# Folding the second entry's w2 on VectorE with operands in PSUM, in a conditioned transformer block on one Trainium2 core

## The chip, the core and the metric

The kernel runs on one core of a Trainium2 chip. The core has TensorE (matrix products into PSUM), VectorE (element-wise steps and the reads that add a product to its destination), ScalarE, called ACT in the profile (activations and copies), GpSimd, called POOL (element-wise sums in SBUF), and SyncE, called SP, which issues transfers. The metric is the device time of one execution in microseconds.

## The reference

For two batch entries of 2048 rows with 512 features, everything in f32:

```
emb = silu(t) @ ada_w + ada_b                 # six rows of 512 for each batch entry
shift_msa, scale_msa, gate_msa, shift_mlp, scale_mlp, gate_mlp = split(emb, 6)
norm = ln(x) * (1 + scale_msa) + shift_msa
h    = gelu(norm @ ssm_w1 + ssm_b1)           # 512 x 512, the error-function gelu
x    = x + gate_msa * (h @ ssm_w2 + ssm_b2)   # 512 x 512
n2   = ln(x) * (1 + scale_mlp) + shift_mlp
hf   = gelu(n2 @ ff_w1 + ff_b1)               # 512 x 1024, the tanh gelu
x    = x + gate_mlp * (hf @ ff_w2 + ff_b2)    # 1024 x 512
```

## The kernel before, in words

The 4096 rows are cut into eight blocks of 512 rows, numbered 0 to 7; blocks 0 to 3 belong to the first batch entry, 4 to 7 to the second. Each block passes four products, named in the tiles: hA (norm by w1, then gelu), oA (by w2, added to x), hC (n2 by fw1, then gelu) and oC (by fw2, added to x). The order of the work on each engine is the order in which the Python code issues it. Around block i the stages come as hC_i ("products"), oA_{i+1}, oC_i, hA_{i+2}, and then hC_{i+1}.

Every product is computed with fewer multiplications at the price of sums: a matrix is cut into quarters 11, 12, 21, 22, seven products P1 to P7 of quarters or sums of quarters are formed, and their results are added into the quarters of the output. `sums_of_second` (lines 397 to 404) forms four such sums for a right-hand weight: s0 = 12 - 11, s1 = 22 - s0, 12 = 22 - 12 and s2 = 21 - s1. For the hC products of later blocks a longer program is used: `HK_B` lists twenty sums of the sixteen input registers of n2 ("forms"), `HK_P` the 26 products in their order, each with the PSUM bank that it uses and the outputs that read it. In `HK_B` GpSimd forms most sums (L1184); those named in `beside` are formed by VectorE (L1180), one operand of each having been copied to PSUM by ACT (L773, `copied_registers`, one tile for register pair 3 and, if register 17 is among them, one for pair 1).

Work that isn't a matrix product is hung into the product stages by `hook(hooks, places, ops)`: after the product at a place has been issued and its result's read has been issued, the steps hooked there are issued. In `group` the places are named "P1", "P2", "P6", "P5", "P7", "P3", "P4" and count the seven positions in that order. The hA groups of blocks 3 and later, which are called with the order `CARRIED`, compute P1, P5, P6, P2, P7, P3, P4 in these positions, so steps hooked at "P5" follow the product P2. hA_0 uses the order `FIRST` and its places carry the products' own names: P1, P2, P5, P6, P7, P3, P4. In the 26 products of hC the places are the numbers of the products; in `residual_in_all_leaves` (oC of blocks 2, 3 and 5) they are "0a", "0b" to "6a", "6b", the two halves of seven rounds.

In a CARRIED hA group P1 goes to a PSUM bank "y", which ACT copies to a bank "x" (L564); P5 and P6 are read by ACT (L814), P2 by ACT with gelu (L824), P7 by VectorE into its destination (L833) and then ACT with gelu (L834), P3 by VectorE (L836) and ACT (L837), and P4 by ACT (L840). P1, P6, P7 and P4 accumulate in the same bank "y", so each of them has to wait for the read of the one before.

The gate of each batch entry is multiplied into the weight instead of the output. For w2 and the second entry this happens around block 2 (`refold2`; i = 2, which is also one of the blocks in `SEVEN`): w2 is loaded anew at "0a" of oC_2 (`load_w`), the gate row (`gsb_2_1`, loaded during oA_3) is copied into a PSUM tile by ACT (`take_gate`, L374) at "P5" of hA_4, and four folds (L434, VectorE, one 128x512 slice of w2 each, the other operand the gate in PSUM) are hooked at "P5", "P7", "P3" and "P4"; `sums_of_second` follows on GpSimd at "P4" (L386). At "P5" the row of b2 is loaded into the buffer that the gate row had (`gate_bias`), and during hC_3, at products 5, 8 and 12, three VectorE steps multiply it by the gate (L1158, L1159, L1160). w2's new operands are first read in oA_4.

Two LayerNorm steps of later blocks are touched too. `sums_on_act` gives the row sums of block i+3 as four ACT activations with an accumulator (L604), each followed by a short accumulator read; `squares_on_act` (L616) gives the squares during the next block's hC products; `root` forms `ve` on VectorE (L640) and then r = ve to the power of -1/2 on GpSimd (L641); `steps` refines r on VectorE (L681 to L689). In hA_0 the batch statistics of one quarter of block 1 are taken on VectorE (`mixed_stats`, L587 and L588), the rest on ACT.

The PSUM pool `ps_t` has two buffers; the register copies, the gate and the small tile of `steps` come from it.

Of the kernel before, what the change touches and what calls it, by code (L numbers as in the profile page):

```python
# [36 lines left out]
F32 = mybir.dt.float32  # L37
AF = mybir.ActivationFunctionType
ALU = mybir.AluOpType
# [101 lines left out]
def kernel(  # L141
# [196 lines left out]
    def gate_rows_of(g):  # L338
        pa = rows_of(g)
        r = w2_t[:, 2 * P : 3 * P] if g == 2 else w2_t[:, 3 * P : 4 * P]  # L340
        nc.vector.tensor_tensor(r, pa[:, :P], gate_b[g], ALU.add)
        gate_rows[g] = r
# [28 lines left out]
    def take_gate(g, b):  # L371

        pg = ps_t.tile([P, D], F32, tag="t", name=f"pgate_{g}_{b}")
        nc.scalar.copy(pg, gate_rows[g, b])  # L374
        gate[g, b] = pg
# [53 lines left out]
    def weight_of_second(w_sb, s, gt, engs, cut=1, sum_eng=nc.gpsimd):  # L429

        K = w_sb.shape[1]

        def fold(k):
            engs[k % len(engs)].tensor_tensor(w_sb[:, k, :], w_sb[:, k, :], gt() if callable(gt) else gt, ALU.mult)  # L434

        ops = [lambda k=k: fold(k) for k in range(K)]
        lo, hi = w_sb[:, : K // 2, :], w_sb[:, K // 2 :, :]
        q = {
            "11": lo[:, :, : D // 2],
            "12": lo[:, :, D // 2 :],  # L440
            "21": hi[:, :, : D // 2],
            "22": hi[:, :, D // 2 :],
        }
        s = thirds(s)
        return second_operands(q, s), ops + sums_of_second(q, s, sum_eng, cut)

    pair_t = fw2_t[:, :2].rearrange("p a s k d -> p (a s k d)").rearrange(
        "p (s k q d) -> p s k q d", s=3, k=KD // 2, q=2
    )
# [118 lines left out]
    def hook(hooks, places, ops):  # L568

        for n, op in enumerate(ops):  # L570
            hooks.setdefault(places[min(n, len(places) - 1)], []).append(op)


    class Norm:
# [192 lines left out]
        def copied_registers(self, ks):  # L767


            copied = {}  # L770
            for k in ks:
                t = ps_t.tile([P, C, 2, HT // C], F32, tag="t", name=f"copy{self.name}_{k}")
                nc.scalar.copy(t, self.nT[:, :, k * P : (k + 1) * P].rearrange("p a (h r) -> p a h r", h=2))  # L773
                copied |= {2 * k + col: t[:, :, col] for col in range(2)}
            return copied
# [569 lines left out]
    def run(ops):  # L1345
        for op in ops:
            op()
# [89 lines left out]
    hook(hooks, ("P1",), n1_sums[2:3])  # L1437
    on_act, on_dve = n1[1].mixed_stats()
    hook(hooks, ("P1",), on_act)
    hook(hooks, ("P2",), on_dve)  # L1440
    hook(hooks, ("P6",), [n1[1].root, lambda: gate_rows_of(2)] + n1_sums[3:])
    hook(hooks, ("P6",), [n1[1].rest] + [lambda c=c: n1[1].normal(c) for c in range(2)])
    hook(hooks, ("P7",), [ssm_gate, gb2_0, lambda: seed("oA_0", b2_bc, 0), lambda: apart_row(b2_bc, nc.gpsimd)] + fold2(0, 1))
    hook(hooks, ("P3",), fold2(1, 2) + [lambda: n1[1].turn(0)] + fold2(2, 4))
# [151 lines left out]
    for i in range(1, NBLK):  # L1596
# [36 lines left out]
            hook(hooks, (17, 19, 21, 23), [lambda c=c: n2[i + 1].turn(c) for c in range(C)])  # L1633
            hook(hooks, (23,), [n2[i + 1].move])
        if nx2 and i > 1:
            hook(hooks, (0,) if ahead else (7,) if unread_stats else (2,), [n1[i + 2].root])
            at = (3, 3, 4, 4, 5, 6) if ahead else (11, 12, 12, 13, 13, 14) if unread_stats else (8, 9, 10, 11, 12, 13)
            hook(hooks, at, n1[i + 2].steps())
        if i == 2:
# [121 lines left out]
        if refold2:  # L1761
            b = (i + 2) // PER_B
            hook(hooks, ("0a",) if seven else ("P1",), [lambda: load_w("w2", w2, w2_sb)])
            w2_ops, w2_fold = weight_of_second(w2_sb, w2_s, (lambda: gate[2, b]) if seven else gate_rows[2, b], (nc.vector,))
            if not seven:
                hook(hooks, ("R2", "R4", "R4", "P3"), w2_fold[:KD])
        if ahead:
            hook(hooks, ("0a",) if seven else ("P1",), [lambda: load_x(i + 2)])
# [16 lines left out]
        if nxt:  # L1785
            def form(engs, beside=()):

                fb[i + 1] = n2[i + 1].registers()
                copied = n2[i + 1].copied_registers((3, 1) if 17 in beside else (3,)) if beside else None
                return sums_of_registers(HK_B, fb[i + 1], engs, copied, beside)  # L1790
# [14 lines left out]
        if not last:  # L1805
            store(i, 1)
        if nx2:
            begin = lambda: run(form((nc.gpsimd,), (19, 12, 7) if refold5 else (19, 17, 12, 11, 2, 7)))
        else:
            begin = lambda: None  # L1810

# [15 lines left out]
            hook(hooks, ("P5",) * 6 + ("P7", "P7", "P3"), folds)  # L1827
        if refold2:
            def bias_2():
                take_gate(2, b)  # L1830
                gb[2], multiply_2 = gate_bias(2, b, b2, f"gb2_{b}")
                return multiply_2()

            found["gb2"] = None
            hook(hooks, ("P5",), [lambda: found.update(gb2=bias_2())])
            if seven:
                hook(hooks, ("P5", "P7", "P3", "P4"), w2_fold[:KD])
            hook(hooks, ("P4",), w2_fold[KD:])
            late_bias = [lambda n=n: found["gb2"][n]() for n in range(3)]
            w2_leaf, late_sums = leaves_of_w2(w2_sb, w2_s, (nc.gpsimd, nc.gpsimd))  # L1840
        unread_stats = []
        if i + 3 < NBLK:
            on_act = i + 4 < NBLK
            st = n1[i + 3].sums_on_act() if on_act else n1[i + 3].stats()
            unread_stats = n1[i + 3].squares_on_act() if on_act else []
            hook(hooks, ("P7", "P7", "P4") if refold5 else ("P5", "P7", "P3", "P4"), st)
        if ahead:
            n2[i + 2] = Norm(i + 2, 2)
            last_stats = n2[i + 2].stats()
# [50 lines left out]
```

## Time and profile before

| | |
|---|---|
| median of 3 runs | 582.67 us (582.5 to 582.76) |
| profiled execution | 582.45 us, its span 580.7 us |
| TensorE busy | 572.8 us (99%) |
| VectorE busy | 450.8 us (78%) |
| GpSimd busy | 435.9 us (75%) |
| ACT busy | 292.5 us (50%) |
| mean granted TensorE clock | 0.998 of full speed |

The span is the time from the first to the last instruction; the rest of the execution's time lies around it. Times in rows of the profile count from the span's start, in microseconds unless marked ns. In a row of a timeline the first number is the start, the second how long the merged instructions lasted, then come engine, line of the kernel, operation, output and inputs, and in brackets the idle time of the engine before it with what ended it. In a row of the chain of waits stand start, length, engine, output and line; DVEq, ACTq and SPq are the instruction queues of VectorE, ACT and SyncE. In a row of groups stand the busy time and the mean ns of one, then the idle time before them. A matrix product x8 is one of the seven products of a group: eight matmuls of 128x256.

### The profile page before, as it was taken

The numbers are of one execution on the slowest core, as the hardware profiler recorded it, in microseconds if no ns is written. First come the engines' busy times: TensorE is split into PE (matmuls) and PEld (weight loads), VectorE is DVE, ScalarE is ACT, GpSimd is POOL, SyncE is SP. The second block draws the span as 40 slices with busy tenths as digits, with TensorE's granted clock in tenths as the row PEclk, the third lists the DMA queues.
The fourth block names the chain that finished last, engine by engine and source line by source line (L and its number), as shares of the span: only waits on it lengthen the run. The fifth ranks groups of instructions, "written<-read, shape, count | busy, mean of one in ns | idle before, by whom it ended". The sixth has DMA issues, their size and how long they took to land.

```text
span 580.7 us, 10061 instructions
## 1 busy us (share of the span) xinstructions
PE 572.8 (99%) x3425; PEld 514.1 (89%) x3425; DVE 450.8 (78%) x954; ACT 292.5 (50%) x573; POOL 435.9 (75%) x453
## 2 busy tenths in 40 slices
PE   8999999999999999999999999999999999999997
PEld 4888888888899889998899988998889998899896
DVE  4968898986878586975869877986757597887677
ACT  3727457705652875448734588335655332741520
POOL 1665449999949879789998989998993955369351
PEclk9999999999999999999999999999999999999999
DMA  8977333204205403373032921243230250031002
GB/s 332 388 220 251 99 74 90 92 37 145 61 14 156 169 40 74 104 241 128 1 91 54 338 98 24 51 122 125 82 108 2 109 145 2 1 74 72 1 2 72
DMA packets 26831, 62.30 MB, mean 107 GB/s; under 512 B 5104, under 2 KB 6172, under 8 KB 25116
## 3 DMA queue, kind: packets, MB, share of 16 engines
q1 hardware_dynamic: 22768, 55.87, 29.7%
q10 hardware_dynamic: 4012, 5.79, 3.9%
q8 instruction: 27, 0.44, 0.3%
q14 instruction: 24, 0.20, 0.1%
HBM read 35.94 MB, written 9.97 MB: 79 GB/s over the span
## 4 chain that ended last, share of the span: by engine, by line
PE 92%; DVE 4%; DMA 2%; issue 1%; ACT 0%; SPq 0%; DVEq 0%; ACTq 0%
PE px_hC L1260 10%; PE py_hA L550 9%; PE pv_hC L1260 8%; PE py_hC L1260 8%; PE py_oA L550 5%; PE py_oC L973 5%; PE pv_hA L550 4%; PE pl_oC_P_y L1021 4%; PE pl_oC_A_y L1111 4%; PE py_oA L908 4%; PE pl_oC_B_y L1111 3%; PE py_hC L550 2%; PE pv_oA L550 2%; PE py_oC L550 2%; PE pl_oC_P_v L1021 2%; PE px_hA L550 2%
## 5 line engine op out<-in xcount | busy, mean ns | idle before, releaser
L641 POOL TENSOR_TENSOR r<-ve,minus_half 128x4 f32<-128x4 f32 x16 | 17.2, 1074 | 53.6 <-DVE ve L640 46.6
L752 ACT ACTIVATE nT<-nT,mod,mod 128x512 f32<-128x512 f32 x32 | 23.4, 803 | 46.1 <-DMA nT<-blocks 32.0
L1184 POOL TENSOR_TENSOR forms<-forms 128x256 f32<-128x256 f32 x56 | 42.1, 751 | 4.2 <-DVE forms L1180 0.7
L1260 PE MATMUL py_hC<-forms,fw 128*128 128x256 f32 x168 | 41.2, 380 | 0.5 <-DVE hClo L1277 0.5
L1277 DVE TENSOR_TENSOR hClo<-hClo,py_hC 128x512 f32<-128x512 f32 x42 | 28.5, 684 | 10.5 <-ACT hClo L1274 8.2
L704 ACT ACTIVATE nT<-x,nmr,rstd 128x512 f32<-128x512 f32 x36 | 26.8, 804 | 19.5 <-DVE nmr L689 16.9
L1260 PEld LDWEIGHTS py_hC<-forms,fw 128*128 128x128 f32 x168 | 31.6, 190 | 5.5 <-DVE hClo L1277 1.2
L386 POOL TENSOR_TENSOR hSC<-hClo,hChi 128x512 f32<-128x512 f32 (+1 forms) x16 | 19.2, 1206 | 20.7 <-ACT hChi L1255 19.1
L587 DVE BATCH_NORM_STATS2 st<-x 128x6 f32<-128x512 f32 x42 | 28.4, 675 | 4.9 <-DMA x<-in_x_dram 4.8
L1277 DVE TENSOR_TENSOR hChi<-hChi,pv_hC 128x512 f32<-128x512 f32 x35 | 23.2, 679 | 10.8 <-ACT hChi L1274 5.1
L1255 ACT ACTIVATE hClo<-hClo,colsT 128x256 f32<-128x256 f32 x56 | 25.3, 498 | 5.3 <-DVE hClo L1277 5.1
L1260 PE MATMUL px_hC<-forms,fw 128*128 128x256 f32 x112 | 27.6, 379 | 0.0
L752 ACT ACTIVATE x<-x,mod 128x512 f32<-128x512 f32 x24 | 17.6, 802 | 19.1 <-DMA x<-blocks 19.1
L715 DVE STREAM_TRANSPOSE blocks<-nT 128x512 f32<-128x512 f32 x36 | 24.2, 694 | 2.8 <-ACT nT L704 2.8
L386 POOL TENSOR_TENSOR hClo<-hClo 128x512 f32<-128x512 f32 (+1 forms) x23 | 26.1, 1137 | 0.0
L1255 ACT ACTIVATE hChi<-hChi,colsT 128x256 f32<-128x256 f32 x56 | 25.1, 495 | 1.9 <-DVE hChi L1277 1.9
L1274 ACT ACTIVATE hChi<-py_hC 128x512 f32<-128x512 f32 x14 | 7.6, 595 | 34.3 <-PE py_hC L1260 34.2
L1260 PEld LDWEIGHTS px_hC<-forms,fw 128*128 128x128 f32 x112 | 21.3, 190 | 2.9
L1274 ACT ACTIVATE hClo<-px_hC 128x512 f32<-128x512 f32 x21 | 12.5, 596 | 22.2 <-PE px_hC L1260 18.6
L550 PE MATMUL py_hA<-x,w 128*128 128x256 f32 x96 | 22.7, 379 | 0.0
L1277 DVE TENSOR_TENSOR hChi<-hChi,px_hC 128x512 f32<-128x512 f32 x28 | 19.0, 680 | 4.5 <-ACT hClo L1274 2.1
L1260 PE MATMUL px_hC<-forms,fw_s 128*128 128x256 f32 x84 | 20.7, 381 | 0.0
(513 smaller groups left out, 1913.2 us busy)
## 6 DMA issues: line engine op xcount, KB each, us to landing
x<-in_x_dram SPq DMA_DIRECT2D x13, 1024.0 KB
out_dram<-x SPq DMA_DIRECT2D x14, 512.0 KB
x<-blocks SPq DMA_DIRECT2D x96, 64.0 KB
nT<-blocks SPq DMA_DIRECT2D x88, 64.0 KB
ada<-in_L_cond_ada_w_dram SPq DMA_DIRECT2D x5, 1024.0 KB
fw<-in_L_cond_ff_w_dram SPq DMA_DIRECT2D x2, 2048.0 KB
nT<-blocks ACTq DMA_DIRECT2D x56, 64.0 KB
w<-in_L_cond_ssm_w_dram SPq DMA_DIRECT2D x2, 1024.0 KB
```

Of the source, the lines that this page charges most:

```text
L386: eng.tensor_tensor(out[:, r], a[:, r], b[:, r], f)
L550: nc.tensor.matmul(ps[b][j * apart][:, j, :], lhs(p, j, k), rhs(p, j, k), start=(fresh and j * (not apart) == 0 and k == 0), stop=(p in (" ...
L587: nc.vector.bn_stats(st, xs[self.i][:, c, :])
L704: nc.scalar.activation(t, x_c, AF.Identity, bias=self.nmr[:, c : c + 1], scale=self.rstd[:, c : c + 1])
L752: nc.scalar.activation(dst, src, AF.Identity, bias=shift, scale=scale)
L973: yield lambda j=j, k=k: nc.tensor.matmul(ps[BANK[p]][:, j, :], hops(p, j, k), wops[p][:, k, :], start=False, stop=(k == kdim - 1), skip_g ...
L1021: nc.tensor.matmul(t[:, n, :], hops.leaves[p][f][:, k, :], leaf_wops[p][f][:, k, :], start=room not in started, stop=(f in ("P2", "P3", "P ...
L1111: nc.tensor.matmul(rooms[g, b][:, at[p], :], hops.leaves[p][f][:, k, :], leaf_wops[p][f][:, k, :], start=(g, b) not in started, stop=(f in ...
L1184: eng.tensor_tensor(reg[d], reg[a], reg[b], ALU.add if f == "+" else ALU.subtract)
L1255: nc.scalar.activation(h, h, AF.Gelu_apprx_tanh, bias=fb1T[:, m : m + 1])
L1260: nc.tensor.matmul(ps[b][:, j, :], fa[ra][:, j * P : (j + 1) * P], fb[rb].rearrange("p a (c q) -> p c a q", q=Q), start=(fresh and j == 0) ...
L1277: nc.vector.tensor_tensor(dest(d), dest(d), ps[b], op)
```

## The change

All of it concerns the refold of w2 for the second entry, and two LayerNorm steps.

- `take_gate` for this refold is hooked at "5b" of oC_2, one stage earlier than "P5" of hA_4.
- The folds go by quarters of w2 in the order 12, 11, 22, 21, all four hooked at "P1" of hA_4. The fold of 12 writes its result into the PSUM tile that held the register copies (`room`); the others write in place.
- The four sums move from GpSimd to VectorE, each with one operand in `room`: s0 = room - 11 and 12 = 22 - room at "P5"; ACT then copies 22 into `room` at "P7", s1 = room - s0 follows at "P3"; ACT copies 21 into `room` at "P3", and s2 = room - s1 follows at "P4".
- Of the sums in `HK_B` for block 3, registers 19, 12 and 7 stay on VectorE; 17, 11 and 2 go to GpSimd, and only one register copy is made.
- ACT's four row sums for block 5 are hooked at "P2", "P6", "P5", "P7" of hA_4 in place of "P5", "P7", "P3", "P4".
- `root` of blocks 4 and 5, in the hC products of blocks 2 and 3, moves from product 7 to product 9, behind the reads of products 8 and 9.
- In hA_0 the VectorE batch statistics of block 1 move from "P2" to the head of "P6", behind the reads of P5 and P6.

```diff
+    def weight_beside(w_sb, s, gt, room):
+
+        K, F, s = w_sb.shape[1] // 2, D // 2, thirds(s)
+        h = w_sb.rearrange("p (h k) (q f) -> p h q k f", h=2, q=2)
+        q = {f"{j + 1}{n + 1}": h[:, j, n] for j in range(2) for n in range(2)}
+
+        def fold(n):
+            out = room() if n == "12" else q[n]
+            c = slice(0, F) if n[1] == "1" else slice(F, D)
+            nc.vector.tensor_tensor(out, q[n], gt()[:, c].unsqueeze(1).to_broadcast([P, K, F]), ALU.mult)
+
+        def beside(out, a, b):
+            return lambda: nc.vector.tensor_tensor(out, a or room(), b or room(), ALU.subtract)
+
+        def copied(n):
+            return lambda: nc.scalar.copy(room(), q[n])
+
+        sums = [beside(s[0], None, q["11"]), beside(q["12"], q["22"], None), copied("22"), beside(s[1], None, s[0])]
+        sums += [copied("21"), beside(s[2], None, s[1])]
+        return second_operands(q, s), [lambda n=n: fold(n) for n in ("12", "11", "22", "21")], sums
...
-                t = ps_t.tile([P, C, 2, HT // C], F32, tag="t", name=f"copy{self.name}_{k}")
+                t = found["copies"] = ps_t.tile([P, C, 2, HT // C], F32, tag="t", name=f"copy{self.name}_{k}")
...
-    hook(hooks, ("P2",), on_dve)
-    hook(hooks, ("P6",), [n1[1].root, lambda: gate_rows_of(2)] + n1_sums[3:])
+    hook(hooks, ("P6",), on_dve + [n1[1].root, lambda: gate_rows_of(2)] + n1_sums[3:])
...
-            hook(hooks, (0,) if ahead else (7,) if unread_stats else (2,), [n1[i + 2].root])
+            hook(hooks, (0,) if ahead else (9,) if unread_stats and not fold else (7,) if unread_stats else (2,), [n1[i + 2].root])
...
-            w2_ops, w2_fold = weight_of_second(w2_sb, w2_s, (lambda: gate[2, b]) if seven else gate_rows[2, b], (nc.vector,))
-            if not seven:
+            if seven:
+                hook(hooks, ("5b",), [lambda: take_gate(2, b)])
+            if seven:
+                room = lambda: found["copies"].rearrange("p a h r -> p (a h r)").rearrange("p (k f) -> p k f", k=KD // 2)
+                w2_ops, w2_fold, w2_sums = weight_beside(w2_sb, w2_s, lambda: gate[2, b], room)
+            else:
+                w2_ops, w2_fold = weight_of_second(w2_sb, w2_s, gate_rows[2, b], (nc.vector,))
...
-            begin = lambda: run(form((nc.gpsimd,), (19, 12, 7) if refold5 else (19, 17, 12, 11, 2, 7)))
+            begin = lambda: run(form((nc.gpsimd,), (19, 12, 7) if refold5 or refold2 else (19, 17, 12, 11, 2, 7)))
...
             def bias_2():
-                take_gate(2, b)
+                if not seven:
+                    take_gate(2, b)
...
             if seven:
-                hook(hooks, ("P5", "P7", "P3", "P4"), w2_fold[:KD])
-            hook(hooks, ("P4",), w2_fold[KD:])
+                hook(hooks, ("P1",), w2_fold)
+                hook(hooks, ("P5", "P5", "P7", "P3", "P3", "P4"), w2_sums)
+            else:
+                hook(hooks, ("P4",), w2_fold[KD:])
...
-            hook(hooks, ("P7", "P7", "P4") if refold5 else ("P5", "P7", "P3", "P4"), st)
+            hook(hooks, ("P7", "P7", "P4") if refold5 else ("P2", "P6", "P5", "P7") if refold2 else ("P5", "P7", "P3", "P4"), st)
```

## Prediction, made before the changed kernel ran

> **What bounds the kernel now.** I read the page first, then TensorE's own waits, then the chain of waits, and only then the timelines of the places that the chain names.
>
> ```profile
> span 580.7 us, 10061 instructions
> PE 572.8 (99%) x3425; PEld 514.1 (89%) x3425; DVE 450.8 (78%) x954; ACT 292.5 (50%) x573; POOL 435.9 (75%) x453
> ...
> PE py_hA L550 <- DVE hA L833: 0.7, 1, 0.7
> ...
> PE py_hC L1260 <- DVE hClo L1277: 0.5, 1, 0.5
> PE py_hA L550 <- DVE ve L640: 0.2, 1, 0.2
> ```
>
> TensorE is busy for 572.8 of 580.7 us, so only moments in which it stands still can be won. Three of its five waits are for VectorE, once each, and each lies where this change edits. The chain shows the first two (start, length, what):
>
> ```profile
> 259.84 1.74 PE px_hA L550 x8
> ...
> 262.95 0.84 ACT hA L824 x2
> 263.79 0.50 ACT pgate L374
> ...
> 264.31 0.69 DVE w L434
> 264.99 0.61 DVE hA L833
> ...
> 265.74 1.96 PE py_hA L550 x8
> ...
> 275.25 0.71 ACT unread L616 x2
> ...
> 275.98 0.03 DVE ve L640
> ...
> 276.85 0.67 DVE hClo L1277
> ...
> 279.59 0.61 DVE hClo L1277
> ...
> 280.25 1.13 PE py_hC L1260 x4
> ```
>
> First place, the hA_4 product group: P2's gelu waits on ACT for a table load, the gate copy (L374) stands behind it, the first fold of w2 (L434) waits for the copy at the head of VectorE's queue, and behind the fold waits the read of P7's bank (L833), which TensorE needs before P4. Second place, the hC_3 products: the variance step `ve` (L640) waits for ACT's last square, and the reads behind it run late until TensorE waits for one at 280.25. What both cost is read by setting these stages beside the same stages one block earlier, which have the same TensorE work:
>
> ```profile
> 186.65 1.73 PE py_hA L550 x8
> ...
> 200.46 1.73 PE px_hC L1260 x8
> ...
> 221.18 1.73 PE py_oA L908 x8
> ...
> 254.66 1.73 PE py_hA L550 x8
> ...
> 269.43 1.73 PE px_hC L1260 x8
> ...
> 290.91 1.73 PE py_oA L908 x8
> ```
>
> hA: 269.43-254.66 = 14.77 against 200.46-186.65 = 13.81, so 0.96 us lost. hC products: 290.91-269.43 = 21.48 against 221.18-200.46 = 20.72, so 0.76 lost. The third place is hA_0; its idle time stands in the row:
>
> ```profile
> 20.15 0.68 DVE L587 BATCH_NORM_STATS2 st<-x 128x6 f32<-128x512 f32 x1
> ...
> 21.54 0.68 DVE L816 TENSOR_TENSOR forms<-py_hA,colsT 128x512 f32<-128x512 f32 x1
> ...
> 22.36 1.97 PE L550 MATMUL py_hA<-nT,w 128*128 128x256 f32 x8 [0.25 <-DVE ve L640]
> ```
>
> It is put down to `ve`, but what P7 needs is the read of P6's bank (L816), which ends at 22.22 and ran late behind the batch statistics of 20.15. Everything the change could win is thus 0.96 + 0.76 + 0.25 = 1.97 us.
>
> **The change part by part.** Prices first:
>
> ```profile
> L434 DVE TENSOR_TENSOR w<-w,pgate 128x512 f32<-128x512 f32 x4 | 2.6, 678 | 3.9 <-ACT pgate L374 3.9
> ...
> L386 POOL TENSOR_TENSOR w_s<-w,w_s 128x512 f32<-128x512 f32 x2 | 2.5, 1271 | 0.1
> ...
> L1184 POOL TENSOR_TENSOR forms<-forms 128x256 f32<-128x256 f32 x8 | 5.8, 729 | 0.5
> ...
> L386 DVE TENSOR_TENSOR nS<-nT x1: 1296/1296/1296, 15.0 to 15.0; 128x512 f32<-128x512 f32 x1
> ...
> 266.71 1.27 DVE L434 TENSOR_TENSOR w<-w,pgate 128x512 f32<-128x512 f32 x2
> ```
>
> A 128x512 step with one operand in PSUM lasts 0.68 us, and since two take 1.27, a queue of them moves on every 0.60.
>
> *Gate copy to "5b".* One ACT copy of 0.50 leaves the place between the gelu and the folds. It now follows the four modulations of n2, which ACT spends idle time waiting for:
>
> ```profile
> 253.12 2.93 ACT L752 ACTIVATE nT<-nT,mod,mod 128x512 f32<-128x512 f32 x4 [7.38 <-DMA nT<-blocks]
> ...
> 258.38 1.42 DVE L1180 TENSOR_TENSOR forms<-copy,forms 128x256 f32<-128x256 f32 x4 [2.20 <-POOL forms L1184]
> ...
> 264.30 0.34 SPq L227 DMA_DIRECT2D gb<-in_L_cond_ssm_b_dram  x1
> ```
>
> It runs from 256.05 (253.12+2.93) and can push ACT's next step, the copy that P2 adds to, by at most its own 0.50; P2 starts only at 259.84. If that copy were late, P2 would wait; as it stands the edit costs nothing. On SyncE the load of the b2 row (264.30) needs the buffer that the gate copy reads, so it can only leave earlier.
>
> *Folds and sums.* VectorE waits until 258.38 for GpSimd's third form; that stays. Its register sums fall from six to three: 3 x 0.355 (1.42/4), to 259.45. Then four folds (one into PSUM) and two sums, 6 x 0.60, to 263.05. w2's own load is issued in the first round of oC_2, as before, and the gate is there since 256.6. P7 ends near 263.3 (259.84+1.74+1.73), so L833 runs at once, 263.3 to 263.9. P4, were it not held, would start no earlier than 265.74-0.96 = 264.78; it followed L833's end by 0.14 (264.99+0.61 to 265.74), so L833 has to end by 264.64. 0.7 us are to spare; if they were gone, P4 would wait as before. The two late sums wait for ACT's two added copies (0.50 each) and come behind L836; the copies replace two ACT copies (the second register copy and the gate copy's old place). VectorE then has 2.00 us idle to hold the last sum:
>
> ```profile
> 269.98 1.28 DVE L1277 TENSOR_TENSOR hChi<-hChi,pv_hC 128x512 f32<-128x512 f32 x2 [2.00 <-ACT hChi L1274]
> ...
> 275.64 1.27 POOL L386 TENSOR_TENSOR hSA<-hA,hSA 128x512 f32<-128x512 f32 x1
> ```
>
> Gain 0.96. GpSimd loses four sums (4 x 1.27 = 5.1) and takes three register sums (3 x 0.73 = 2.2), so it is 2.9 us ahead afterwards: its hSA sums end near 274.0 instead of 276.9.
>
> The unknown is what a quarter-wise fold and a fold written to PSUM cost. Ends: 0.60 each, the same operands in L434, and 1.25, the 1.296 of L386, whose inputs both lie in SBUF while GpSimd works. I take 0.60, since each of the six has one operand in PSUM and L434 had GpSimd busy beside it. So the sum stands with the first end, and the other end is the first rival.
>
> The Trainium skill, "VectorE: DVE Perf Modes", section "The TRN2 errata", speaks against operands in PSUM: it prices a VectorE step with its source in PSUM at 120 cycles and one for each element, with its source in SBUF at 58 and one for each, at 0.96 GHz. For 512 elements that is 658 ns against 594, an estimate from that page; six steps of 658 ns, none overlapping, would take 3.95 us instead of 3.6, L833 would start at 263.4 and the sum would be the same. The trace differs from both figures: L434 with its PSUM operand lasts 678 ns and its queue moves on every 0.60 us.
>
> *ACT's row sums of block 5 one to two places earlier.* Four activations with accumulator reads, now from about 259.05. They read x_5, so it must have landed:
>
> ```profile
> 252.00:256.75 4.75, 4.75 (x35) 4.49 (x35) 3.76 (x13) 3.25 (x5) 3.04 (x3) 1.00 0.88 333
> ```
>
> 333 GB/s over 4.75 us is 1.58 MB: the parked 0.5 MB and x_5's 1.0 MB. It is there 2 us before. One takes some 0.7 (0.71 for the pair of rows of such a step at 275.25), and ACT waits for TensorE after every product of hA_4, which runs 1.73. No cost; if ACT fell behind, P7 and P4 would wait for its reads of P6's and P5's banks.
>
> *Root behind two reads (blocks 2 and 3).* In hC_3 the read of 276.85 stood behind `ve`:
>
> ```profile
> 207.01 0.17 DVE L640 TENSOR_SCALAR ve<-mv 128x4 f32<-128x4 f32 x1 [0.44 <-ACT unread L616]
> ...
> 207.26 1.02 POOL L641 TENSOR_TENSOR r<-ve,minus_half 128x4 f32<-128x4 f32 x1 [3.62 <-DVE ve L640]
> ...
> 275.98 0.95 DVE L640 TENSOR_SCALAR ve<-mv 128x4 f32<-128x4 f32 x1 [1.05 <-ACT unread L616]
> ```
>
> The same `ve` took 0.17 in block 2 with GpSimd idle, and 0.95 here, ending with GpSimd's sum of 275.64. After the change it follows step 9's read, when the squares are done and GpSimd has been idle since 274.0; no read stands behind the squares any more. Gain 0.76. The price is a later `r`: in block 2 by up to two products (the 1.73 of an x8 row), and GpSimd's sums with it. Their cover is the wait before its next `r`:
>
> ```profile
> 237.24 1.02 POOL L641 TENSOR_TENSOR r<-ve,minus_half 128x4 f32<-128x4 f32 x1 [2.92 <-DVE ve L640]
> ```
>
> Without that cover TensorE would wait for leaf sums in oC_2, at most those 1.73 us.
>
> *Statistics behind P6's read (hA_0).* L816 moves up by the 0.68 and 0.18 in front of it, past P6's end; P7 then follows the 0.25 earlier. `ve` and `r` come some 0.2 later, and with them the normalised rows of block 1, whose first product comes only after all of oA_0. Gain 0.25.
>
> Sum: 0.96 + 0.76 + 0.25 = 1.97. The profiled execution took 582.45 us, 0.22 under the median 582.67 of the runs (582.5 to 582.76): 582.45 - 1.97 = 580.48, and 580.7 on the scale of the median.
>
> **The rivals.** *VectorE arrives late at P7's bank (slower).* If the six new steps cost 1.25 each, they end at 259.45 + 7.5 = 266.95, L833 at 267.6 and P4 starts at 267.7 instead of 265.74: 2.0 worse than before, against 1.0 won at the other two places, so 583.7. P4 is touched from 0.76 us a step, and the whole turns slower from about 1.09 (L833 ending 1.0 later than before, at 266.6). Against it speaks L434; for it, only that no fold of the trace goes by quarters or into PSUM.
>
> *Half of it.* The wait at P4 goes, but VectorE still comes late in hC_3, because `ve` meets GpSimd in the middle of a sum again (the 0.95) or the third bias product and the steps fall together: 0.76 less, 581.4. The Trainium skill, "SBUF — State Buffer", section "Who interferes with whom", holds that a VectorE scalar step in its two-port mode and a GpSimd step lock each other out for a whole instruction; the trace agrees (0.17 with GpSimd idle, 0.95 ending with its sum), and by that rule this case hangs on whether GpSimd's four sums are over by then. If instead P4 keeps part of its wait, 581.2 to 581.7. For it: three bias products lie in that stage that block 2 has not; against it: block 2 has four other VectorE sums there and no wait.
>
> *The gain is given back.* TensorE gets ahead of GpSimd, which is busy 75% of the time, and waits in oC_3 for leaf sums: about 582.5, no change. Against it: GpSimd gains 2.9 us just before, and its next `r` waits for VectorE, 2.92 in block 2.
>
> **How the numbers follow.** Full gain 0.64 (580.5 to 581.0), half 0.18 (581.0 to 581.9), given back 0.06 (near 582.5), slower 0.12 (from 583). The forecast is 580.7; 580.4 to 581.9 takes in the first two cases. About 0.2% (1.2 us) is what a measurement of this kernel can tell: the half gain lies on that border, so faster 0.80, same 0.08, slower 0.12.
>
> **What would show it.** Right: the waits of py_hA for L833, of py_hC for L1277 and of P7 in hA_0 are gone; pgate's copy stands near 256; six VectorE steps of 0.68 lie between 259.4 and 263.1 and L833 starts by 263.5; `ve` of block 5 takes 0.17; hA_4 and the hC_3 products take 13.81 and 20.72. Wrong: steps of over 0.75 us, a new TensorE wait for GpSimd in oC_2 or oC_3, or ACT waiting for x_5.

## The result, and the profile after

The changed kernel takes 580.34 us (median of 6 runs, 580.2 to 580.38) against 582.6 us for the kernel before beside it (6 runs, 582.01 to 583.11): a ratio of 0.9961, with a 95% interval of 0.9948 to 0.9974. It is 2.26 us faster. The forecast was 580.7 us and its range began at 580.4, so the time lies 0.06 us below the range: the direction held and all three places were right, but one term of the sum was too small. The profiled execution of the changed kernel took 580.38 us with a span of 578.6, 2.07 and 2.1 under those of before.

The lines of the kernel that are quoted here and stand behind the new function are 21 higher: L816 is now L837, L833 is L854, L1277 is L1298, L640 is L661. The page's first lines, after:

```profile
span 578.6 us, 10061 instructions
...
PE 572.1 (99%) x3425; PEld 514.2 (89%) x3425; DVE 453.8 (78%) x955; ACT 292.8 (51%) x574; POOL 432.2 (75%) x452
```

TensorE's waits, after (us in total, times, longest):

```profile
PE idle L1390 <- POOL w_t masks.py:199: 1.3, 1, 1.3
PE pada L304 <- DMA ada<-in_L_cond_ada_w_dram: 0.7, 1, 0.7
PE rowsT L1399 <- DMA fw_t<-in_L_cond_ff_b_dram: 0.2, 1, 0.2
```

The three waits for VectorE that the prediction quoted are gone. TensorE's work is the same, 3425 matmuls; it stands still less. What is left are waits at the very start of the kernel, which the change does not touch.

The chain of waits, after, at the three places that the prediction used as its rulers:

```profile
254.27 1.73 PE py_hA L571 x8
...
268.09 1.73 PE px_hC L1281 x8
...
288.81 1.73 PE py_oA L929 x8
```

From hA_4 to the first `px` product of hC_3 are now 268.09 - 254.27 = 13.82 us, where before it was 14.77 and one block earlier 13.81; from there to oA_4 are 288.81 - 268.09 = 20.72, where before it was 21.48 and one block earlier 20.72. Both stages have come down to their undisturbed length, to 0.01 us.

VectorE's timeline in hA_4 after the change (start, length, engine, line, operation, tiles, and in brackets the idle time before):

```profile
259.27 0.70 DVE L456 TENSOR_TENSOR copy<-w,pgate 128x512 f32<-128x512 f32 x1
259.88 1.88 DVE L456 TENSOR_TENSOR w<-w,pgate 128x512 f32<-128x512 f32 x3
261.67 0.68 DVE L459 TENSOR_TENSOR w_s<-copy,w 128x512 f32<-128x512 f32 x1
262.27 0.68 DVE L459 TENSOR_TENSOR w<-w,copy 128x512 f32<-128x512 f32 x1
263.01 0.69 DVE L854 TENSOR_TENSOR hA<-py_hA,hA 128x512 f32<-128x512 f32 x1
...
265.35 0.68 DVE L459 TENSOR_TENSOR w_s<-copy,w_s 128x512 f32<-128x512 f32 x1
266.69 0.69 DVE L459 TENSOR_TENSOR w_s<-copy,w_s 128x512 f32<-128x512 f32 x1 [0.66 <-ACT copy L462]
```

The fold into PSUM lasts 0.70 us and the next starts 0.61 behind it, the three others take 1.88 together, and a sum lasts 0.68 at a pace of 0.60. The first six end at 262.95, and L854 starts at 263.01, as soon as P7 is out. TensorE takes the next products without a gap:

```profile
262.74 1.89 PE L571 MATMUL pv_hA<-x,w_s 128*128 128x256 f32 x8
264.47 1.89 PE L571 MATMUL py_hA<-nS,w 128*128 128x256 f32 x8
266.20 1.03 PE L1281 MATMUL py_hC<-forms,fw_s 128*128 128x256 f32 x4
```

In hC_3, on GpSimd and on VectorE:

```profile
272.26 1.28 POOL L386 TENSOR_TENSOR hSA<-hA,hSA 128x512 f32<-128x512 f32 x1
275.94 1.02 POOL L662 TENSOR_TENSOR r<-ve,minus_half 128x4 f32<-128x4 f32 x1 [2.40 <-DVE ve L661]
```

```profile
275.70 0.16 DVE L661 TENSOR_SCALAR ve<-mv 128x4 f32<-128x4 f32 x1
```

GpSimd's sums end at 273.54 instead of 276.91 (275.64 + 1.27), it then idles for 2.40 us, and `ve` takes 0.16 instead of 0.95.

Third, hA_0, TensorE after the change:

```profile
19.12 1.89 PE L571 MATMUL py_hA<-nS,w_s 128*128 128x256 f32 x8
20.94 1.08 PE L287 MATMUL pada<-ada,w_t 128*32 128x128 f32 x32
21.95 1.99 PE L571 MATMUL py_hA<-nT,w 128*128 128x256 f32 x8
```

P7 (21.95) follows P6 (19.12) by 2.83 us. The rows of P6 and `pada` before:

```profile
19.04 1.89 PE L550 MATMUL py_hA<-nS,w_s 128*128 128x256 f32 x8
21.04 1.08 PE L287 MATMUL pada<-ada,w_t 128*32 128x128 f32 x32
```

P7 followed at 22.36, 3.32 behind P6: 0.49 more, not the 0.25 of the bracket at that row.

By starts of TensorE's products the two profiled executions compare like this (hA_0 to P7 from the starts of hA_0's first product, 13.75 before and 13.84 after; hA_4, hC_3 and oA_4 by their first products, as the timelines have them):

| stretch | before | after | difference |
|---|---|---|---|
| to the start of hA_0 | 13.75 | 13.84 | +0.09 |
| hA_0 to its P7 | 8.61 | 8.11 | -0.50 |
| hA_4 to hC_3 | 13.04 | 12.09 | -0.95 |
| hC_3 to oA_4 | 23.20 | 22.44 | -0.76 |
| oC_4 | 22.91 | 22.94 | +0.03 |

The four differences up to oA_4 add up to -2.12; oA_4 starts at 288.64 instead of 290.74, 2.10 earlier.

### The profile page after: what moved, and what is told of

The parts are those of the page before. It is cut to its first block, busy times and chain, and to the rows that moved or that the text cites. A ratio compares the mean times of both kernels' runs of the same rounds, so it can differ in the third digit from the quotient of the medians.

```text
span 578.6 us, 10061 instructions
## 1 busy us (share of the span) xinstructions
PE 572.1 (99%) x3425; PEld 514.2 (89%) x3425; DVE 453.8 (78%) x955; ACT 292.8 (51%) x574; POOL 432.2 (75%) x452
## 4 chain that ended last, share of the span: by engine, by line
PE 95%; DVE 2%; DMA 2%; issue 0%; SPq 0%; DVEq 0%
PE px_hC L1281 10%; PE py_hA L571 10%; PE py_hC L1281 8%; PE pv_hC L1281 8%; PE py_oA L571 5%; PE py_oC L994 5%; PE pv_hA L571 5%; PE pl_oC_P_y L1042 4%; PE pl_oC_A_y L1132 4%; PE py_oA L929 4%; PE pl_oC_B_y L1132 3%; PE py_hC L571 2%; PE pv_oA L571 2%; PE px_hA L571 2%; PE py_oC L571 2%; PE pl_oC_P_v L1042 2%
## 5 line engine op out<-in xcount | busy, mean ns | idle before, releaser
L1298 DVE TENSOR_TENSOR hClo<-hClo,py_hC 128x512 f32<-128x512 f32 x42 | 28.6, 684 | 11.6 <-ACT hClo L1295 8.2
L1298 DVE TENSOR_TENSOR hChi<-hChi,pv_hC 128x512 f32<-128x512 f32 x35 | 23.2, 680 | 9.4 <-PE pv_hC L1281 5.1
L1298 DVE TENSOR_TENSOR hChi<-hChi,px_hC 128x512 f32<-128x512 f32 x28 | 19.0, 680 | 4.2 <-ACT hClo L1295 2.1
```

The costliest lines, as they stand in the source:

```text
L1298: nc.vector.tensor_tensor(dest(d), dest(d), ps[b], op)
```

## The experiments

Two theories stood at the start. The first is the prediction's: three separate stalls, each removed by one part of the change. The rival: some parts do nothing, and the gain comes from what remains (from GpSimd having less to do, or from the place of the sums alone). The first two experiments add one part to the kernel before, the next five take one part out of the changed kernel. The others are repetitions, for a finding that came up on the way.

### Statistics behind P6's read, alone

```diff
-    hook(hooks, ("P2",), on_dve)
-    hook(hooks, ("P6",), [n1[1].root, lambda: gate_rows_of(2)] + n1_sums[3:])
+    hook(hooks, ("P6",), on_dve + [n1[1].root, lambda: gate_rows_of(2)] + n1_sums[3:])
```

> The kernel before with one part of the change alone: in hA_0 the batch statistics of block 1 go behind the reads of P5 and P6. My theory: P7 no longer waits for P6's late read, and nothing else moves; from the start of P6 to the start of P7 stood 3.32 us before and stand 2.83 in the changed kernel, so 0.3 to 0.5 us are won here and about as much of the whole time. Rival: only the 0.25 of the idle column belongs to the statistics, and the rest of the 0.49 is the arrival of a weight load, which would then vary from run to run: the gates' row products would start anywhere from 1.8 to 2.0 us after P6, whichever kernel runs.

Measured: 582.36 us (581.36 to 583.05) against 582.57 (581.75 to 583.32), ratio 0.9993 (0.9984 to 1.0003). hA_0 to P7 took 8.11 us, as in the changed kernel, so the edit takes the whole 0.50 out of hA_0. But the time does not show it. TensorE's waits in the profiled execution, 582.74 us and so one of the two slowest of the ten:

```profile
PE py_hA L550 <- DVE hA L833: 0.7, 1, 0.7
...
PE pl_oC_P_y L1021 <- DVE fw L386: 0.7, 1, 0.7
PE py_hC L1260 <- DVE hClo L1277: 0.6, 1, 0.6
```

The waits in hA_4 and hC_3 are still there, as they must be, and there is a new one in oC_4, some 365 us later: oC_4 took 23.55 us instead of 22.91. In this execution, what was won in hA_0 was lost there; whether the faster runs lost it too, no profile shows. What this wait is, is told below.

### Root behind two reads, alone

```diff
-            hook(hooks, (0,) if ahead else (7,) if unread_stats else (2,), [n1[i + 2].root])
+            hook(hooks, (0,) if ahead else (9,) if unread_stats and not fold else (7,) if unread_stats else (2,), [n1[i + 2].root])
```

> The kernel before with the root step alone moved from product 7 to product 9 (blocks 2 and 3). My theory of the prediction: the read of product 8 no longer stands behind the squares and behind GpSimd's sum, so the hC_3 products take 20.7 to 20.9 us instead of 21.48 and the whole is 0.6 to 0.76 us faster; hA_4 keeps its 14.77. Rival: what held the reads was GpSimd, busy with its hSA sums until 276.9; a root step at product 9 still meets a sum and takes up to 0.95, so the wait is not won without GpSimd's relief and the hC_3 products stay at 21.2 to 21.5.

Measured: 582.35 us (581.7 to 582.71), ratio 0.9992 (0.9983 to 1.0001); its profiled execution took 581.77. hC_3 to oA_4 lasted 22.44 us: the wait is gone entirely, without any relief for GpSimd. On VectorE and on GpSimd of this execution:

```profile
277.10 0.17 DVE L640 TENSOR_SCALAR ve<-mv 128x4 f32<-128x4 f32 x1
```

```profile
275.98 1.27 POOL L386 TENSOR_TENSOR hSA<-hA,hSA 128x512 f32<-128x512 f32 x1
```

GpSimd's sums end at 277.25, as late as before. `ve` now comes at their very end and takes 0.17, and the reads that used to stand behind it have been issued ahead of it. The median does not show the 0.76: it is 0.22 below the kernel before, and the interval takes in no difference at all. Four of the ten runs lie near 581.8, four near 582.4 and two near 582.7. The repetitions at the end take this up.

### The change without the move of root

```diff
-            hook(hooks, (0,) if ahead else (9,) if unread_stats and not fold else (7,) if unread_stats else (2,), [n1[i + 2].root])
+            hook(hooks, (0,) if ahead else (7,) if unread_stats else (2,), [n1[i + 2].root])
```

> The changed kernel with the root step back at product 7. My theory of the prediction: the step itself waits for ACT's last square there, reads come late, and part of the 0.76 us of the hC_3 products comes back (20.9 to 21.5 us). Rival: since GpSimd is through its hSA sums by 273.5 in the changed kernel, the step takes 0.17 as in block 2, where it stood at product 7 and cost nothing; the hC_3 products stay at 20.72 and the time is that of the changed kernel.

Measured: 580.94 us (580.33 to 581.14), ratio 0.997 (0.9958 to 0.9981). hC_3 to oA_4 lasted 22.44 us here too. GpSimd's last sum of this execution, and `ve`:

```profile
272.31 1.28 POOL L386 TENSOR_TENSOR hSA<-hA,hSA 128x512 f32<-128x512 f32 x1
```

```profile
274.61 0.17 DVE L661 TENSOR_SCALAR ve<-mv 128x4 f32<-128x4 f32 x1 [1.22 <-ACT unread L637]
```

`ve` still waits 1.22 us for the last square, but it no longer meets GpSimd, takes 0.17, and no read behind it is late. It is GpSimd that made the difference to `ve`, which stands 8.43 us behind hC_3's first product (274.61 - 266.18), against 8.44 before (275.98 - 267.54), and takes 0.17 in place of 0.95. So hC_3's 0.76 us can be had in two ways: by the place of `root` (the experiment before) or by relieving GpSimd (this one). In the full change they are redundant in hC_3. The 0.6 us that this kernel is slower than the changed one lie elsewhere: its TensorE waits in oC_4 for `fw`, 0.6 us, and its oC_4 took 23.53 us against 22.94.

### The four sums of w2 back on GpSimd

```diff
-                w2_ops, w2_fold, w2_sums = weight_beside(w2_sb, w2_s, lambda: gate[2, b], room)
+                w2_ops, w2_fold = weight_of_second(w2_sb, w2_s, lambda: gate[2, b], (nc.vector,))
...
-                hook(hooks, ("P1",), w2_fold)
-                hook(hooks, ("P5", "P5", "P7", "P3", "P3", "P4"), w2_sums)
+                hook(hooks, ("P1",), w2_fold[:KD])
+                hook(hooks, ("P4",), w2_fold[KD:])
```

The four folds stay at "P1" of hA_4, by slices and in place; GpSimd keeps the three register sums that the change gave it.

> The changed kernel with the gate early and the four folds at P1 on VectorE, but the four sums of w2 on GpSimd as before, at P4. My theory: the wait at P4 of hA_4 is gone all the same, since it hung on the gate's copy (13.81 us); but GpSimd now has three register sums more and is 2.2 us later than before, ends its hSA sums near 279 and forms r at 279 to 280, and VectorE's LayerNorm steps at product 12 wait for that, so the hC_3 products lose 1 to 2.5 us against 20.72. Rival: GpSimd's lateness is hidden, the hC_3 products stay within 0.2 of 20.72, and the whole time is that of the changed kernel: then taking the sums off GpSimd bought nothing.

Measured: 582.34 us (581.58 to 582.75), ratio 0.9997 (0.9987 to 1.0006). hA_4 to hC_3 is 12.09 us, as in the changed kernel: for P4 the gate's earlier copy and the earlier folds suffice. But hC_3 to oA_4 is 23.29, 0.85 more. TensorE's waits, then GpSimd and VectorE:

```profile
PE py_hC L1281 <- DVE hClo L1298: 0.6, 1, 0.6
...
PE px_hC L1281 <- DVE hChi L1298: 0.2, 1, 0.2
```

```profile
278.29 1.01 POOL L662 TENSOR_TENSOR r<-ve,minus_half 128x4 f32<-128x4 f32 x1
```

```profile
279.34 0.17 DVE L706 TENSOR_TENSOR small<-r,small 128x4 f32<-128x4 f32 x1 [1.40 <-POOL r L662]
```

One wait has taken the place of another: `ve` is out in time, but `r` stands behind GpSimd's sums until 278.29, the step of VectorE that uses `r` blocks its queue for 1.40 us, and the reads behind that step are late. The 0.85 is less than the 1 to 2.5 that was expected. The move of the sums is what pays for the three register sums on GpSimd; without that part the median is not measurably below the kernel before. The profile explains only a part of this: 0.85 here and another 0.35 in hC_6, where a read of VectorE starts late without a wait that the trace names. The profiled execution itself took 581.68, near the fastest of the ten; what the slower ones carried is not shown.

### The sums on VectorE, but wholly in SBUF

```diff
-                w2_ops, w2_fold, w2_sums = weight_beside(w2_sb, w2_s, lambda: gate[2, b], room)
+                w2_ops, w2_fold = weight_of_second(w2_sb, w2_s, lambda: gate[2, b], (nc.vector,), 1, nc.vector)
...
-                hook(hooks, ("P1",), w2_fold)
-                hook(hooks, ("P5", "P5", "P7", "P3", "P3", "P4"), w2_sums)
+                hook(hooks, ("P1",), w2_fold[:KD])
+                hook(hooks, ("P5", "P5", "P3", "P4"), w2_fold[KD:])
```

> The changed kernel with the four sums of w2 on VectorE as they are, but both operands in SBUF: 12 is folded in place, and ACT copies nothing. My theory, that a VectorE step with two SBUF inputs waits for GpSimd's running sum: the sums take 1.0 to 1.6 us each instead of 0.68; two of them stand before the read of P7's bank, which then starts 0.7 to 1.5 late, and P4 of hA_4 waits 0.3 to 1.2 us (hA_4 at 14.1 to 15.0 instead of 13.81); GpSimd's own sums may lengthen too. Rival: the operands' place does not matter, the sums take 0.68, hA_4 stays at 13.81, and the PSUM room and the two copies are needless.

Measured: 580.38 us (580.25 to 580.66) against 582.43, ratio 0.9967 (0.9955 to 0.998): the time of the changed kernel, with two ACT copies less. VectorE, then GpSimd's last hSA sum, this kernel:

```profile
261.55 0.80 DVE L386 TENSOR_TENSOR w_s<-w 128x512 f32<-128x512 f32 x1
262.38 1.10 DVE L386 TENSOR_TENSOR w_s<-w,w_s 128x512 f32<-128x512 f32 x1
263.41 0.68 DVE L854 TENSOR_TENSOR hA<-py_hA,hA 128x512 f32<-128x512 f32 x1
...
265.47 1.21 DVE L386 TENSOR_TENSOR w<-w 128x512 f32<-128x512 f32 x1
266.60 1.21 DVE L386 TENSOR_TENSOR w_s<-w,w_s 128x512 f32<-128x512 f32 x1
...
273.67 1.28 POOL L386 TENSOR_TENSOR hSA<-hA,hSA 128x512 f32<-128x512 f32 x1
```

With both operands in SBUF the sums take 0.80 to 1.21 us instead of 0.68, and GpSimd slows too: the last of its four hSA sums ends at 274.95 instead of 273.54. L854 starts 0.40 later, P4 follows 0.25 late (hA_4 to hC_3 12.34 instead of 12.09). The contention costs 0.25 us at one place of this profile, less than the 0.3 to 1.2 that was expected, and the medians (580.38 and 580.34) do not show even that. So it is not the place of the operands in PSUM that won the 2.26 us; what counted is that the sums left GpSimd (580.38 with them on VectorE and in SBUF, 582.34 with them on GpSimd). The Trainium skill, "SBUF — State Buffer", section "Who interferes with whom", says that a VectorE step contends with GpSimd's reads when both its inputs lie in SBUF, and outside its two-port modes does not when at most one does; these rows agree (0.80 to 1.21 against 0.68).

### The statistics back at "P2"

```diff
-    hook(hooks, ("P6",), on_dve + [n1[1].root, lambda: gate_rows_of(2)] + n1_sums[3:])
+    hook(hooks, ("P2",), on_dve)
+    hook(hooks, ("P6",), [n1[1].root, lambda: gate_rows_of(2)] + n1_sums[3:])
```

> The changed kernel with the batch statistics of block 1 back at P2 of hA_0. My theory: 0.3 to 0.5 us are lost, all of it between P6 and P7 of hA_0 (3.3 us from start to start). Rival: 0.25 or less is lost, and the gates' row products start 1.8 us after P6 as in the changed kernel, so that part of what the two first profiles differ by was chance.

Measured: 580.71 us (580.58 to 581.24), ratio 0.9973 (0.9964 to 0.9982), 0.37 above the changed kernel's median. TensorE in hA_0:

```profile
21.10 1.08 PE L287 MATMUL pada<-ada,w_t 128*32 128x128 f32 x32
22.57 1.97 PE L571 MATMUL py_hA<-nT,w 128*128 128x256 f32 x8 [0.39 <-DVE ve L661]
```

The same place as before the change, but the bracket now says 0.39, and hA_0 to P7 is 8.57 us, 0.46 above the 8.11 of the changed kernel. The term is about 0.5, not 0.25.

### ACT's row sums back at "P5", "P7", "P3", "P4"

```diff
-            hook(hooks, ("P7", "P7", "P4") if refold5 else ("P2", "P6", "P5", "P7") if refold2 else ("P5", "P7", "P3", "P4"), st)
+            hook(hooks, ("P7", "P7", "P4") if refold5 else ("P5", "P7", "P3", "P4"), st)
```

> The changed kernel with ACT's four row sums of block 5 back at P5, P7, P3 and P4 of hA_4. My theory: with ACT's two copies now in the same stage, ACT ends the stage about 1.4 us later (two of four row sums of 0.7 lie behind P2 instead of before it), its first reads of the hC_3 products come late by as much, and the products lose 0.2 to 1 us. Rival: ACT's first reads were 0.8 us late before as well without any wait of TensorE, the products stay at 20.72, and the place of the row sums is free.

Measured: 580.52 us (580.43 to 580.85), ratio 0.9969 (0.9958 to 0.998). hC_3 to oA_4 is 22.69, 0.25 more than in the changed kernel. ACT in this kernel, around the last read of hA_4 (L861):

```profile
267.51 0.82 ACT L861 ACTIVATE hA<-py_hA,colsT 128x256 f32<-128x256 f32 x2
268.22 0.62 ACT L625 ACTIVATE unread<-x 128x512 f32<-128x512 f32 x1
...
268.83 1.08 ACT L1295 ACTIVATE hChi<-py_hC 128x512 f32<-128x512 f32 x2
```

And in the changed kernel:

```profile
266.59 0.83 ACT L861 ACTIVATE hA<-py_hA,colsT 128x256 f32<-128x256 f32 x2
267.32 1.09 ACT L1295 ACTIVATE hChi<-py_hC 128x512 f32<-128x512 f32 x2
```

The last row sum stands between L861 and ACT's first read of hC_3, which comes 1.51 us later (268.83 against 267.32; this execution as a whole ran 0.29 later there). The two copies of w2's quarters have taken the room that the row sums had in ACT's queue. Moving the row sums is therefore no free rider: it keeps 0.25 us.

### Repetitions: who is first at a sum in oC_4

oC_4 lasted 22.9 us in seven of the nine profiles so far and 23.5 in two, and the difference was one VectorE sum, `fw`, beside one of GpSimd. In the changed kernel, VectorE, then GpSimd:

```profile
385.64 0.41 DVE L386 TENSOR_TENSOR fw<-fw 128x256 f32<-128x256 f32 x1
```

```profile
384.46 1.27 POOL L386 TENSOR_TENSOR forms<-hSC,forms 128x512 f32<-128x512 f32 x1
385.70 0.94 POOL L386 TENSOR_TENSOR forms<-hClo,forms 128x256 f32<-128x256 f32 x1
```

In the kernel with the statistics moved alone:

```profile
387.34 1.05 DVE L386 TENSOR_TENSOR fw<-fw 128x256 f32<-128x256 f32 x1
```

```profile
386.14 1.29 POOL L386 TENSOR_TENSOR forms<-hSC,forms 128x512 f32<-128x512 f32 x1
387.38 0.74 POOL L386 TENSOR_TENSOR forms<-hClo,forms 128x256 f32<-128x256 f32 x1
```

In both, `fw` starts just before GpSimd's next sum. In the first VectorE has its 0.41 us and GpSimd's sum is stretched to 0.94; in the second GpSimd has its 0.74 and `fw` is stretched to 1.05. Which of the two the order favours is read here from these lengths. `fw` starts 1.18 us after GpSimd's previous sum did in the one (385.64 - 384.46), 1.20 in the other (387.34 - 386.14). The kernel before was therefore profiled three times more, unchanged, and the kernel with the statistics alone once more.

> The kernel before, unchanged, profiled once more. In the profiles so far oC_4 took 22.9 us where VectorE's sum `fw` of 128x256 took 0.41 us and 23.5 where it took 1.05, beside the same sum of GpSimd; the start of the two lay within 0.1 us. Theory: which engine is first there is settled anew in each execution, by a few hundredths of a us. Then the executions of one kernel differ in it: `fw` takes 0.4 or 1.05 and nothing between, oC_4 22.9 or 23.5, and the time is about 582.45 with 0.4 and about 583.1 with 1.05. In hC_3 `ve` meets GpSimd's sum in the same way, so a time near 581.8 would be an execution in which it does not: `ve` 0.17 and hA_4 to oA_4 0.7 shorter. Rival: the order is fixed by the program; then `fw` takes 0.41 in this kernel every time, hA_4 to oA_4 lasts 36.24, and what spreads is the start of hA_0 (13.7 to 14.2 so far) and the granted clock.

> The kernel before, unchanged, a second repetition. Theory: `fw` 0.4 or 1.05 from one execution to the next, oC_4 22.9 or 23.5, time 582.45 or 583.1, or near 581.8 where `ve` of hC_3 takes 0.17. Rival: `fw` 0.41 and oC_4 22.9 every time, the spread of the time from the start of hA_0 and the clock.

> The kernel before, unchanged, a third repetition. Theory: `fw` 0.4 or 1.05 from one execution to the next, oC_4 22.9 or 23.5, time 582.45 or 583.1, or near 581.8 where `ve` of hC_3 takes 0.17. Rival: `fw` 0.41 and oC_4 22.9 every time, the spread of the time from the start of hA_0 and the clock.

> The kernel before with the batch statistics behind P6's read alone, profiled once more; its first profile showed `fw` at 1.05 us and oC_4 at 23.55, at a time of 582.74. Theory (settled anew in each execution): `fw` 0.41, oC_4 22.9 and a time of about 582.1 are as possible as 1.05, 23.5 and 582.7. Rival (fixed by the program): 1.05 and 23.5 again, near 582.7.

Measured: 582.45, 582.45 and 585.05 us for the kernel before, with `fw` at 0.41 in all three and oC_4 at 22.9; 583.0 for the statistics alone, with `fw` at 1.04 again. The rival is right as far as profiles show: the order belongs to the program, not to the execution, and it holds even where the whole execution is shifted. The third repetition shows one source of spread: a weight load at the start came late, these products began 1.25 us later than in the first profile (10.41 against 9.16), and hA_0 2.5 later (16.25 against 13.75):

```profile
10.41 1.08 PE L304 MATMUL pada<-ada,w_t 128*32 128x128 f32 x32 [1.70 <-DMA ada<-in_L_cond_ada_w_dram]
```

Last, the kernel with `root` moved alone three times more:

> The kernel before with `root` at product 9 alone, profiled once more. Its first profile showed no wait in hC_3, `fw` at 0.41 us and 581.77, but the median of its ten runs was 582.35, with four near 581.8, four near 582.4 and two near 582.7. Theory: in this kernel the order of `fw` and GpSimd's sum in oC_4 differs from one execution to the next: times near 581.8 have `fw` 0.41 and oC_4 22.9, times near 582.4 have 1.05 and 23.55, and hA_4 to oA_4 is 35.5 in both. Rival: the order is fixed by the program, oC_4 is 22.9 every time, and times near 582.4 have a later start of hA_0 (14.3 in place of 13.82) or a wait elsewhere.

> The same kernel, a second repetition. Theory: near 581.8 with `fw` 0.41 and oC_4 22.9, or near 582.4 with 1.05 and 23.55. Rival: oC_4 22.9 every time; a time near 582.4 comes with a later start of hA_0 or a wait elsewhere.

> The same kernel, a third repetition. Theory: near 581.8 with `fw` 0.41 and oC_4 22.9, or near 582.4 with 1.05 and 23.55. Rival: oC_4 22.9 every time; a time near 582.4 comes with a later start of hA_0 or a wait elsewhere.

Measured: 581.68, 581.63 and 581.72 us, `fw` 0.41 in all, no wait in hC_3. With the first that is four profiles between 581.63 and 581.77, against 582.45 in three of four of the kernel before: alone, the move of `root` is worth 0.7 to 0.8 us in profiles. What the runs near 582.4 of the earlier comparison carried, no profile has caught; that stays open. The groups lie some 0.6 us apart, which is what `fw` costs, and of the six runs without the move of `root` one took 580.33, as little as the changed kernel: so it is not excluded that in runs without a profile the order differs after all. What, in the program, decides the order at `fw` is open too: in the two kernels that have the statistics moved and `root` at product 7 (the first and the third experiment) it is `fw` that is stretched, in the others, the kernel before and the changed one among them, it is GpSimd's sum. That `root`'s place acts on it is shown by the kernels; by which path is not.

## Why the prediction missed its range by a little

*hA_4, 0.96.* Right: 0.95. The fold price of 0.60 held for the fold by quarters too; the one into PSUM lasted 0.70, and the next stood 0.61 behind it. The six steps ended at 262.95, L854 started at 263.01 where "263.5" was the bound, and its end at 263.70 left 0.77 us to P4's start; less the 0.14 that P4 needs behind it, the slack is 0.63 where the prediction had 0.7. SyncE's load of the b2 row did move forward (from 264.30 to 256.57) and cost nothing. The gate's earlier copy and the four folds at "P1" are enough for this stage, as the kernel with the sums back on GpSimd shows; the two were not tried apart. Nor was the move of the three register sums: by an estimate, 3 x 0.355 = 1.07 us more on VectorE would have used up the 0.63.

*hC_3, 0.76.* Right in size, and 20.72 to the last digit; incomplete in cause. The prediction let the place of `root` and GpSimd's relief work together. Either alone removes the wait. And the move of ACT's row sums, which it put at "no cost" and gave no gain, is needed for the whole 0.76: without it 0.25 comes back. The later `r` cost nothing, as said; what a really late `r` costs is shown by the kernel with the sums back on GpSimd, 0.85.

*hA_0, 0.25.* This is the step that failed: the mechanism is right, the term was mis-sized, and measured 0.49. The prediction read the idle time in front of P7, `[0.25 <-DVE ve L640]`, as all that P6's late read costs, though by its own account that read moves up by 0.68 and 0.18, past P6's end. But between P6 and P7 stand the gate rows' products `pada`, and in that execution they too started late, 2.00 us behind P6's start (21.04 - 19.04) instead of the 1.82 of the changed kernel (20.94 - 19.12). A second profile of the same kernel names their wait:

```profile
21.10 1.08 PE L287 MATMUL pada<-ada,w_t 128*32 128x128 f32 x32 [0.20 <-DMA ada<-in_L_cond_ada_w_dram]
22.37 1.97 PE L550 MATMUL py_hA<-nT,w 128*128 128x256 f32 x8 [0.19 <-DVE ve L640]
```

There they waited for a load, inside the time that TensorE would have waited for P6's read anyway. So the bracket showed what the load had left over. Where the load came in time (the kernel with `root` alone, the one with the statistics put back) the same wait shows as 0.40 and 0.39. The stage's length tells it without any bracket: 8.57 to 8.71 in the nine profiles with the statistics at "P2", 8.11 or 8.12 in the seven with them behind the reads.

Up to 0.18 of the 0.49 may be luck. In six of the nine profiles with the statistics at "P2" `pada` starts 1.94 to 2.09 us behind P6; in the other three, and in all seven with the statistics behind the reads, it starts after 1.82, with the load on time. What decides when the load lands, the profiles do not show. With `pada` on time on both sides 0.46 is won (8.57 against 8.11). Had it started as late after the change as in the profile of before, P7 would have followed at 22.05 (21.04 + 1.01) instead of 22.36, by an estimate from these rows, and 0.31 would have been won.

*From the span to the median.* The prediction added 0.22 us because the median of three runs lay that much above the profiled execution. That distance does not carry over: the medians of the kernel before lay between 582.43 and 582.67 in the four series of runs beside which the others were measured, two further profiles of it gave 582.45 again, the third 585.05 with a late load, and the changed kernel's median lies 0.04 below its profile. So of the 0.36 us between the forecast 580.7 and 580.34, 0.24 are the term of hA_0 and 0.22 this step, less 0.09 for the later start of hA_0 and the 0.01 by which hA_4 gained less. By the profiled execution's own scale the corrected sum is 582.45 - 0.95 - 0.76 - 0.49 + 0.09 (the later start of hA_0) = 580.34, against 580.38 in the profile.

*The range.* It reached from the sum far upward, to the half gain, but downward only 0.08 below 580.48. It took no bound for a term being too small, though the row that carried the third term was itself put down to the wrong step (`ve`, as the prediction noticed). The row of the read itself gave a bound: L816 started at 21.54, 0.61 us behind P6's end at 20.93 (19.04 + 1.89). With 0.61 as the upper end of the third term, the 0.24 would have been inside.

*The rivals.* VectorE late at P7's bank: excluded by the rows of hA_4; even with all operands in SBUF the price was 0.25 us, not 2.0. Half of it: `ve` did not meet GpSimd, and with `root` left at product 7 it did not either. The gain given back through GpSimd in oC_3: TensorE shows no such wait in this kernel. When the four sums stay on GpSimd a part is given back, but in hC_3, by way of `r`.

## What to carry to other kernels

Size a stall by the length of the whole stage against an undisturbed twin, not by the idle time printed before one instruction: another wait on the same engine may have run inside it, and what is won then hangs also on whether that other wait comes again. When an engine is relieved in one queue, look at what the replaced work does in the next (here ACT's two copies, which needed the row sums out of their way). And where two engines start on SBUF within some hundredths of a microsecond, as at `fw`, a change far away can turn which of them is stretched, and hide or feign a gain of its own size, so judge a part of a change by its stages as well as by its time.

## What the runs showed of the hardware

The VectorE sum `fw` of 128x256, with both operands in SBUF, took either 0.41 or 1.04 to 1.05 us beside GpSimd, nothing between, in all sixteen profiles of this case, with `fw` starting 1.17 to 1.20 us behind GpSimd's previous sum in every one of them. One of the two is stretched: GpSimd's 0.73 became 0.93 to 0.97 in the one case, VectorE's 0.41 became 1.04 to 1.05 in the other, and only the second reaches TensorE, with 0.6 us. Unexpected was that each program gave the same order in every profile taken of it (four of four, four of four and two of two), and that moving a statistics step at 20 us turned it at 387. The Trainium skill, "SBUF — State Buffer", section "Who interferes with whom", says that the order of issue decides who blocks. These rows cannot bear it out: by the starts recorded, `fw` comes 0.03 to 0.07 us before GpSimd's sum in all sixteen profiles, whichever of the two is stretched. What decides it in one program and another, no run here shows.
